# Three seams between the layers of a four-layer attention kernel, held banks for the statistics, and the order of the last tokens' products

## The chip, the cores and the metric

The kernel runs on one core of a Trainium2 chip. Its time is the device time of one execution in microseconds (us): the median of three runs is given, and a profile of one further execution. Engines are called as in the profile: PE (TensorE), DVE (VectorE), ACT (ScalarE), POOL (GpSimd), SP (the queue that issues DMAs).

## What is computed

The input x is four images of 56 x 56 pixels with 256 channels, float32. Four layers follow one another, each x = x + mixer(gn(x)), where gn is a group normalisation over 32 groups of channels and all pixels of an image. The core of the reference, cut:

```python
# layer 0: every pixel attends to its 7x7 neighbours, zero padding, 8 heads of 32
logits = einsum('ndhw,ndkhw->nkhw', q, unfold(k)) * scale
out = einsum('nkhw,ndkhw->ndhw', softmax(logits), unfold(v)) ; out @ wo.T + bo
# layer 1: all 3136 pixels of an image against each other
A = exp(5 * (xn xn' - rowmax)); A = A * (1 - eye); A = A / A.sum(-1)
diff = rowsum * (x W_aff) - (A x) W_aff ; leaky(layernorm(diff))
# layer 2: 7x7 neighbourhood attention clamped at the borders, 4 heads with
# dilation 1 and 4 with dilation 2, a relative position bias per head
# layer 3: attention within 7x7 windows of the image shifted by 3 pixels,
# a relative position bias and a mask of -100 between parts that don't touch
```

## The kernel before

The layers run one after another over all four images; the residual stream and the values go through DRAM between them. The kernel proper is the function `direct_blocks`. Layer 0 takes the span's first 712 us, layer 1 until about 2580, layer 2 until about 3238, layer 3 the rest. Near the end of a layer its units carry steps of the next one, as "fill".

**Who sets the order.** In layers 0 and 2 a scheduler orders the instructions of every engine by their dependences, unless an `issue_after` ties one to another. In layer 1 the order on PE and DVE, in layer 3 that on PE, DVE, ACT and POOL, is the order of the code (`manual_schedule`, called in `run`, L2304). SP issues its DMAs from one queue.

**Attention units, layers 0 and 2** (`attend_pairs`, L1062). A unit is a group of query pixels with all 8 heads. PE makes the logits (L1075) in two halves s0 and s1; DVE adds mask or bias to the one (L1082) and ACT takes its exp (L1083); ACT takes the exp of the other (L1085) and POOL multiplies it by the mask's exp (L1086). The next turn of the loop then issues, for the unit before ("held"): `both`, in which POOL adds the two key halves into b (L1095); the fill steps; the products (L1104): e with the values vp, then b with a matrix of ones for the sums; and `done`: a reciprocal on DVE, ACT's watch of it (`no`, L998), and the multiplication into attn on DVE (L1263, L1977 to L1983). The products go into a PSUM bank with tag o (two banks), which `gather` takes when the unit is made, before its logits; the gather also issues the DMAs of vp (L1967 in layer 2). Sixteen products of 32 columns count as x32 in the timeline.

**Rows.** Layer 0 has 32 rows r, each of seven pixel rows of an image and four units (`stream`, L1293; `balanced`, L1054, spreads the steps over them); the last three rows carry the first tokens of layer 1 instead. Layer 2 has 16 rows r of fourteen pixel rows and eight units: four column groups i, each with m = 0 and m = 1 (`stream`, L2014). Each row projects the row before (`project_out`; PE L952, DVE L2008 and L896) and prepares the next one: `normalise_act` (L942) on ACT or `normalise` (L945) on DVE, projections of queries and keys (L952), values (`value_tiles`, L979, evacuated at L983).

**Statistics** of the group norm (`group_stats`, L901): DVE aggregates (L910), PE sums over the group's channels (`mean`, L914), ACT squares and copies, PE sums again (`scale`, L921 and L922), POOL takes the root. `step_stats` issues one of these steps per unit. Their PSUM columns are 508 to 511 of `spare[0]`, the o bank that the newest unit has just taken; where `spare` is empty, a bank with tag m.

**First tokens of layer 1** (`first_tokens`, L1357). The first image's pixels in seven parts go through load, normal, lengths, values and unit_length; `plan` (L1419) puts these into the fill of layer 0's last three rows, thirteen lists.

**Last tokens of layer 1.** 3136 is 24 blocks of 128 and 64 more. These 64 against the rest are made by `rest_products` (L1609), three units per image; L1615 multiplies on 64 rows of the array, L1619 on 64 columns. PSUM tags in layer 1: s0, s1, o (2 banks), v (2), m (1), t (1). `add_up` evacuates a v bank.

**Masks of layer 3** (`table_steps`, L2060) are made within layer 2: four masks, each two DVE adds (L2072) of `found`, which is gathered by DMA, an exp on ACT (L2074) and one or three stores to DRAM (m3d).

**Layer 3** (`layer3`, L2091) loads the weights and m3, prepares row 0 and 1, makes both rows' values (three blocks of L979 each, in two steps), projects row 0, prepares row 2 and enters its loop `attend_quads` (L1004).

Of the kernel before, what the change touches and what calls it, by code (L numbers as in the profile page):

```python
# [24 lines left out]
FP = mybir.dt.float32  # L25
# [805 lines left out]
def direct_blocks(ctx: ExitStack, tc: tile.TileContext, d: dict, watch):  # L831
# [69 lines left out]
    def group_stats(l, b):  # L901
# [10 lines left out]
        def mean():  # L912
            pm = spare[0][:, 508:510] if spare else ps_m()
# [5 lines left out]
        def scale():  # L919
            pm = spare[0][:, 510:512] if spare else ps_m()  # L920
# [48 lines left out]
    def value_tiles(v, a, c, n, xn, w, bias, dst):  # L969

        t0, t1 = c * n // P, (c + 1) * n // P if (c + 1) * n < T else -(-T // P)
        pm = ps_m()
        sizes = [min(P, T - t * P) for t in range(t0, t1)]
        mine = sizes[2 * a:2 * a + 2]
        for j, k in enumerate(mine):
            first = (2 * a + j) * P
            for h in range(CC):
                for i in range(0, k, HD):
                    nc.tensor.matmul(pm[i:i + HD, j * C:(j + 1) * C], lhsT=xn[:, h, first + i:first + i + HD], rhs=w[:, h, :],  # L979
                                     start=(h == 0), stop=(h == CC - 1))  # L980
        for k in sorted(set(mine)):
# [72 lines left out]
    def balanced(units, steps, free):  # L1054

        n = len(units)
        for i, w in enumerate(units):
            mine = free[i] + steps[i * len(steps) // n:(i + 1) * len(steps) // n]
            w["fill"] = lambda mine=mine: [f() for f in mine]
            yield w  # L1060

    def attend_pairs(pool, units):  # L1062
# [4 lines left out]
        def logits(w):  # L1067
# [9 lines left out]
            for a in range(2):  # L1077
# [3 lines left out]
                if a == 0:  # L1081
                    newest[:] = [nc.vector.tensor_tensor(parts(ev), parts(sv), w["mask"], ALU.add)]  # L1082
                    nc.scalar.activation(ev, ev, AF.Exp)  # L1083
# [5 lines left out]
        def both(w):  # L1089

            nk, nq = w["nk"], w["nq"]
# [6 lines left out]
        def products(w):  # L1098
            nk, nq = w["nk"], w["nq"]
            for k in range(2):  # L1100
                for i, (_, _, v) in enumerate(w["quads"]):
                    for u in range(2 - k):
                        for j in range(4):
                            nc.tensor.matmul(  # L1104
                                w["o"](k, i)[j * HD:(j + 1) * HD], lhsT=ones[:nk, :HD] if k else v(j, u),
                                rhs=w["b"][j // 2][:nk, j % 2, i * nq:(i + 1) * nq] if k else
                                w["e"][j // 2][:nk, j % 2, (2 * i + u) * nq:(2 * i + u + 1) * nq],
                                start=(u == 0), stop=(u == 1 - k))

        held = None  # L1110
        for w in units:
# [4 lines left out]
            if held:  # L1116
                products(held)
                held["done"]()
            held = w
        both(held)  # L1120
        products(held)
# [21 lines left out]
    def layer0(early, big, pool, begin_layer1):  # L1143
# [85 lines left out]
        def pair(r, t):  # L1229
# [11 lines left out]
            def gather():  # L1241
                box["o"] = psum_tile("o", 2)
                spare[:] = [box["o"]]
# [24 lines left out]
            def quad(hq):  # L1268
                def keys(j, u):
# [6 lines left out]
                 for a in range(2)]  # L1276
            return dict(quads=[quad(0), quad(1)], nk=nk, nq=nq, mask=m[0], emask=m[1], first=gather, done=finish,
                        o=lambda k, i: box["o"][:, (2 * i + k) * nq:(2 * i + k + 1) * nq])
# [14 lines left out]
        def stream():  # L1293
# [10 lines left out]
            for r in range(NIMG * NB0):  # L1304
# [8 lines left out]
                if g > 2 or g == 0:  # L1313
                    for i in range(3):
                        free[i].insert(0, step_stats)
                attns[r] = pool.tile([P, CC, BT], FP, tag="attn", name="attn0")
                if r < ALONE:
                    yield from balanced([pair(r, t) for t in range(NTC)], steps, free)
                    continue
# [37 lines left out]
    def first_tokens(few, keep, brief):  # L1357
# [5 lines left out]
        nc.vector.memset(xw[:, :, C:], -1.0)  # L1363
# [14 lines left out]
        def normal(c):  # L1378
            m, n, x = part(c)
            sq = box["sq"] = brief.tile([P, CC, 512], FP, tag="sq", name="sq1")  # L1380
            for h in range(CC):
                normalise_act(x[:, h], x[:, h], known(1, 0), h)
# [25 lines left out]
        def unit_length(c):  # L1408
# [7 lines left out]

        v0, v2 = lambda c: values(c, 0), lambda c: values(c, 2)
# [3 lines left out]
            [(load, 1), (normal, R)],  # L1421
            [(load, 2), (lengths, R), (normal, 0)],
            [(load, 3), (v0, R), (unit_length, R), (lengths, 0)],
            [(v0, 0), (normal, 1), (v2, 0)],
            [(load, 4), (unit_length, 0), (lengths, 1)],
            [(v0, 1), (normal, 2)],
            [(load, 5), (v2, 1), (unit_length, 1), (lengths, 2)],
            [(v0, 2), (normal, 3), (v2, 2)],
            [(unit_length, 2), (lengths, 3)],
            [(v0, 3), (normal, 4)],  # L1430
# [4 lines left out]
    def layer1(early, big, pool, first, late, next_layer):  # L1435
# [173 lines left out]
        def rest_products(b, q, e, own, at):  # L1609
            po = psum_tile("o", 2)  # L1610
            for i in range(4):
                pv = [psum_tile("v", 2) for a in range(2)]
                for a in range(2):
                    half = slice(a * REST, (a + 1) * REST)
                    nc.tensor.matmul(pv[a][:, :C + 1], lhsT=e[half, i * P:(i + 1) * P], rhs=xw[half, NB, :], start=True, stop=True)  # L1615
                for a in range(2):
# [812 lines left out]
```

## Time and profile before

| | us |
|---|---|
| median of 3 runs (lowest, highest) | 3749.66 (3749.12, 3750.91) |
| profiled execution | 3749.95 |
| its span, first to last instruction | 3748.2 |
| mean granted PE clock, of full | 0.996 |
| PE idle in gaps of 0.4 us and more | 80.1, of it 13.6 before the first matmul |
| DMA | 304.94 MB, 81 GB/s |

Lines of the timeline have the start from the span's beginning, the duration from the first to the last of a run of like instructions, the engine and source line, output and inputs by name, the count, and in brackets the idle time of the engine before, with the instruction that ended it. Float32 matmuls leave two records each. Ends of matmuls are modelled, so durations of neighbours overlap a little.

### The profile page before, as it was taken

The numbers are of one execution on the slowest core, as the hardware profiler recorded it, in microseconds if no ns is written. First come the engines' busy times: TensorE is split into PE (matmuls) and PEld (weight loads), VectorE is DVE, ScalarE is ACT, GpSimd is POOL, SyncE is SP. The second block draws the span as 40 slices with busy tenths as digits, with TensorE's granted clock in tenths as the row PEclk, the third lists the DMA queues.
The fourth block names the chain that finished last, engine by engine and source line by source line (L and its number), as shares of the span: only waits on it lengthen the run. The fifth ranks groups of instructions, "written<-read, shape, count | busy, mean of one in ns | idle before, by whom it ended". The sixth has DMA issues, their size and how long they took to land. (4 is left out here: it accounts for less than half of the span.)

```text
span 3748.2 us, 112333 instructions
## 1 busy us (share of the span) xinstructions
PE 3658.8 (98%) x48826; PEld 2477.5 (66%) x48826; DVE 2203.5 (59%) x4188; ACT 1472.0 (39%) x3125; POOL 1812.2 (48%) x1966
## 2 busy tenths in 40 slices
PE   8999999999999999999999999999999999999998
PEld 4666666677776777767777667775666666555554
DVE  5787776544445444554444643445776777777776
ACT  5666666322222222222222222223666666444443
POOL 4777787522234222352222511123777777555555
PEclk9999999999999999999999999999999999999999
DMA  6554444300011000100000000002444444544443
GB/s 224 165 162 135 134 130 139 114 7 24 23 29 35 16 19 19 29 28 23 19 19 24 30 10 10 11 20 83 134 133 138 134 129 118 157 128 135 134 132 100
DMA packets 278039, 304.94 MB, mean 81 GB/s; under 512 B 33624, under 2 KB 268764, under 8 KB 277084
## 3 DMA queue, kind: packets, MB, share of 16 engines
q1 hardware_dynamic: 275680, 297.43, 26.1%
q8 instruction: 385, 6.31, 0.7%
q0 software_dynamic: 1568, 0.16, 0.1%
q14 instruction: 118, 0.97, 0.1%
q10 hardware_dynamic: 288, 0.08, 0.0%
HBM read 205.04 MB, written 92.55 MB: 79 GB/s over the span
## 5 line engine op out<-in xcount | busy, mean ns | idle before, releaser
L1576 DVE TENSOR_TENSOR acc<-acc,ps_v 128x257 f32<-128x257 f32 x1104 | 463.5, 422 | 782.2 <-PE ps_v L1654 753.6
L1654 PE MATMUL ps_v<-xw,e 128*128 128x257 f32 x2208 | 611.0, 381 | 3.4 <-DVE xnT L1521 2.2
L1649 PE MATMUL ps_o<-xw,at 128*128 128x257 f32 x2208 | 609.0, 379 | 0.0
L1544 PE MATMUL ps_s<-xnT,xd 128*128 128x512 f32 (+3 forms) x1344 | 571.4, 548 | 3.9 <-DVE xnT L1521 3.9
L1638 ACT COPY at<-ps_t 128x512 f32<-128x512 f32 (+3 forms) x332 | 170.3, 513 | 961.0 <-PE ps_t L1635 960.7
L1654 PEld LDWEIGHTS ps_v<-xw,e 128*128 128x128 f32 x2208 | 413.4, 189 | 144.6 <-issue 83.2
L1095 POOL TENSOR_TENSOR b<-e 126x336 f32<-126x336 f32 (+5 forms) x512 | 498.3, 993 | 6.9
L1649 PEld LDWEIGHTS ps_o<-xw,at 128*128 128x128 f32 x2208 | 419.1, 190 | 60.1
L952 PE MATMUL ps_m<-xn,w_wqkv 128*32 128x392 f32 x4096 | 376.9, 497 | 4.6 <-ACT kE L1908 3.2
L1537 POOL TENSOR_SCALAR xd<-xnT,vec 128x128 f32<-128x128 f32 x192 | 116.0, 613 | 478.3 <-PE ps_s L1544 478.2
L1547 ACT ACTIVATE e<-ps_s 128x512 f32<-128x512 f32 x336 | 185.3, 552 | 355.3 <-PE ps_s L1544 352.1
L1544 PEld LDWEIGHTS ps_s<-xnT,xd 128*128 128x128 f32 x1344 | 225.4, 191 | 141.4 <-issue 126.2
L1086 POOL TENSOR_TENSOR e<-e,m0t 126x672 f32<-126x672 f32 (+3 forms) x128 | 238.6, 1864 | 165.5 <-ACT e L1085 133.2
L1086 POOL TENSOR_TENSOR e<-e,bias 119x784 f32<-119x784 f32 (+5 forms) x128 | 239.6, 1872 | 157.6 <-ACT e L1085 157.1
L1104 PEld LDWEIGHTS ps_o<-e,vp 124*32 124x32 f32 (+3 forms) x8192 | 200.5, 110 | 101.2 <-issue 81.6
L998 ACT ACTIVATE no<-rs 128x168 f32<-128x168 f32 (+2 forms) x256 | 94.0, 367 | 409.8 <-DVE rs L1973 192.2
L952 PEld LDWEIGHTS ps_m<-xn,w_wqkv 128*32 128x32 f32 x4096 | 124.7, 110 | 179.9 <-issue 129.4
L1973 DVE RECIPROCAL rs<-ps_o 128x196 f32<-128x196 f32 (+2 forms) x128 | 175.7, 1372 | 104.1 <-PE ps_o L1104 104.1
L1104 PE MATMUL ps_o<-e,vp 124*32 124x112 f32 (+3 forms) x8192 | 229.8, 248 | 3.5 <-POOL e L1086 2.9
L1083 ACT ACTIVATE e<-e 126x672 f32<-126x672 f32 (+5 forms) x256 | 219.7, 858 | 14.3 <-DVE e L1082 2.1
L1085 ACT ACTIVATE e<-ps_s 126x672 f32<-126x672 f32 (+5 forms) x256 | 206.1, 805 | 5.0 <-PE ps_s L1075 5.0
L979 PE MATMUL ps_m<-w_wqkv,xn 128*32 128x256 f32 x3136 | 196.8, 381 | 2.1 <-DVE v L983 1.6
(223 smaller groups left out, 5952.3 us busy)
## 6 DMA issues: line engine op xcount, KB each, us to landing
x<-xr SPq DMA_DIRECT2D x64, 392.0 KB
x<-in_x SPq DMA_DIRECT2D x53, 448.0 KB
x<-x SPq DMA_DIRECT2D x60, 392.0 KB
xr<-x SPq DMA_DIRECT2D x60, 392.0 KB
vd<-v SPq DMA_DIRECT2D x72, 256.0 KB
xr<-in_x SPq DMA_DIRECT2D x32, 392.0 KB
xr<-x SPq DMA_DIRECT2D x28, 448.0 KB
x<-xr SPq DMA_DIRECT2D x28, 448.0 KB
```

What stands on the lines that cost most here:

```text
L952: nc.tensor.matmul(pm[j * HD:(j + 1) * HD, :n], lhsT=w[:, h, col + j * HD:col + (j + 1) * HD], rhs=rhs(h), start=(h == 0), stop=(h == CC - 1))
L979: nc.tensor.matmul(pm[i:i + HD, j * C:(j + 1) * C], lhsT=xn[:, h, first + i:first + i + HD], rhs=w[:, h, :], start=(h == 0), stop=(h == CC ...
L1083: nc.scalar.activation(ev, ev, AF.Exp)
L1085: nc.scalar.activation(ev, sv, AF.Exp)
L1086: nc.gpsimd.tensor_tensor(parts(ev), parts(ev), w["emask"], ALU.mult)
L1095: nc.gpsimd.tensor_tensor(w["b"][a][:nk, :, :2 * nq].rearrange("p h (i c) -> p h i c", i=2), ev[:, :, :, 0, :], ev[:, :, :, 1, :], ALU.add)
L1104: nc.tensor.matmul(w["o"](k, i)[j * HD:(j + 1) * HD], lhsT=ones[:nk, :HD] if k else v(j, u), rhs=w["b"][j // 2][:nk, j % 2, i * nq:(i + 1) ...
L1544: nc.tensor.matmul(s[:, :n], lhsT=xd[j][:, h, :], rhs=xnT[:, h, first * P:last * P], start=(h == 0), stop=(h == CC - 1))
L1547: nc.scalar.activation(e[:, :n], s[:, :n], AF.Exp, scale=5.0)
L1576: nc.vector.tensor_tensor(acc[:, i, :], acc[:, i, :], pv[:, :C + 1], ALU.add)
L1649: nc.tensor.matmul(out[j][:, :C + 1], lhsT=e[:, col(i)] if i == j else at[:, col(i)], rhs=xw[:, i, :], start=(i == j), stop=(i == NB - 1))
L1654: nc.tensor.matmul(pv[:, :C + 1], lhsT=e[:, col(i)], rhs=xw[:, j, :], start=True, stop=True)
```

## The change

- `group_stats`: mean and scale write columns 508 to 511 of the held unit's o bank, after that unit's products and before its done (`then` and `after` instead of fill steps).
- `alone`: three units of layer 0's last rows and the four m = 1 units of layer 2's last row have no POOL pre-add; their sums are made by 16 instead of 8 matmuls with ones over e.
- `first_tokens`: loads are issued two units before their use, the memset of xw's last column is a step of the plan, normal is tied behind the exp of the newest unit, and later steps are packed into fewer lists.
- `rest_products`: the order of the two kinds of products, and banks t and m beside v.
- `table_steps`: each mask's adds are tied behind the logit add of the row's last unit.
- layer 2 and 3: a new `layer3_ahead` is opened in layer 2. In row 14 (r = n - 2) it loads row 0 of layer 3 and the three parts of w_qkv, normalises rows 0 and 1 on ACT and loads one half of the first mask; row 14 projects out in units 4 to 7 instead of 2, 3, 6, 7. The six value blocks of layer 3's rows 0 and 1 are fill of units 0, 1, 4 and 5 of row 15, and of the tail. Layer 3 itself starts with the gather of row 0.

```diff
 def mean():
-    pm = spare[0][:, 508:510] if spare else ps_m()
+    pm = spare[0](0) if spare else ps_m()
 def scale():
-    pm = spare[0][:, 510:512] if spare else ps_m()
+    pm = spare[0](1) if spare else ps_m()
...
 def both(w):
+    if w.get("alone"):
+        return
 def products(w):
+    alone = w.get("alone")
     for k in range(2):
         for i, (_, _, v) in enumerate(w["quads"]):
-            for u in range(2 - k):
+            n = 1 if k and not alone else 2
+            for u in range(n):
...
     if held:
         products(held)
+        spare[:] = [held["spare"]]
+        for step in w.get("after", ()):
+            step()
+        spare.clear()
         held["done"]()
     held = w
 both(held)
+for step in tail:
+    step()
 products(held)
...
 # layer 0's units
+    alone=r == ALONE - 1 and t == 3 or r == ALONE and t == 2 or r == NIMG * NB0 - 1 and t == 3,
+    spare=lambda i: box["o"][:, 508 + 2 * i:510 + 2 * i],
...
 # first_tokens
-    for h in range(CC):
-        normalise_act(x[:, h], x[:, h], known(1, 0), h)
+    with tc.issue_after(newest[1].ins):
+        for h in range(CC):
+            normalise_act(x[:, h], x[:, h], known(1, 0), h)
...
 plan = [
     [(load, R), (load, 0)],
-    [(load, 1), (normal, R)],
-    [(load, 2), (lengths, R), (normal, 0)],
-    [(load, 3), (v0, R), (unit_length, R), (lengths, 0)],
+    [(load, 1)],
+    [(weights, 0), (load, 2), (normal, R)],
+    [(load, 3), (lengths, R), (normal, 0)],
+    [(v0, R), (unit_length, R), (lengths, 0)],
     [(v0, 0), (normal, 1), (v2, 0)],
-    [(load, 4), (unit_length, 0), (lengths, 1)],
-    [(v0, 1), (normal, 2)],
-    [(load, 5), (v2, 1), (unit_length, 1), (lengths, 2)],
-    [(v0, 2), (normal, 3), (v2, 2)],
-    [(unit_length, 2), (lengths, 3)],
-    [(v0, 3), (normal, 4)],
+    [(load, 4), (unit_length, 0), (lengths, 1), (v0, 1)],
+    [(normal, 2), (v2, 1)],
+    [(load, 5), (unit_length, 1), (lengths, 2), (v0, 2)],
+    [(normal, 3), (v2, 2)],
+    [(unit_length, 2), (lengths, 3), (v0, 3), (normal, 4)],
     [(v2, 3), (unit_length, 3), (lengths, 4), (normal, 5)],
     [(v0, 4), (v2, 4), (unit_length, 4), (lengths, 5), (v0, 5), (v2, 5), (unit_length, 5)]]
...
 def rest_products(b, q, e, own, at):
     po = psum_tile("o", 2)
+    def by_column(i, banks):
+        for a, bank in enumerate(banks):
+            pv = psum_tile(*bank)
+            half = slice(a * REST, (a + 1) * REST)
+            nc.tensor.matmul(pv[:, :C + 1], lhsT=e[half, i * P:(i + 1) * P], rhs=xw[half, NB, :], start=True, stop=True)
+            found.append((i, a, pv))
+    def add():
+        for i, a, pv in found:
+            add_up(b, 8 * q + 4 * a + i, pv, (nc.vector.tensor_copy, nc.scalar.copy)[a])
+        found.clear()
+    found, pair, others = [], [("v", 2)] * 2, [("t", 1), ("m", 1)]
+    by_column(0, pair)
+    by_column(1, others)
+    add()
     for i in range(4):
-        pv = [psum_tile("v", 2) for a in range(2)]
-        for a in range(2):
-            half = slice(a * REST, (a + 1) * REST)
-            nc.tensor.matmul(pv[a][:, :C + 1], lhsT=e[half, i * P:(i + 1) * P], rhs=xw[half, NB, :], start=True, stop=True)
-        for a in range(2):
-            add_up(b, 8 * q + 4 * a + i, pv[a], (nc.vector.tensor_copy, nc.scalar.copy)[a])
         for a in range(2):
             nc.tensor.matmul(po[a * REST:(a + 1) * REST, :C + 1], ...)
-        tick()
+        if i % 2:
+            tick()
+    by_column(2, others)
+    by_column(3, pair)
+    add()
+    for _ in range(2):
+        tick()
...
 # layer 2's rows
+    if r == n - 4:
+        q[n - 2], q[n - 1] = begin_layer3(0)
 if r:
-    for u, step in zip((2, 3, 6, 7), project_out(r - 1)):
+    for u, step in zip((4, 5, 6, 7) if r == n - 2 else (2, 3, 6, 7), project_out(r - 1)):
         work[u].append(step)
-for u in (1, 4, 5):
-    work[u].insert(0, step_stats)
+if r == n - 2:
+    work[4].append(begin)
+    for u in range(1, 4):
+        work[4 + u].append(lambda u=u: steps3[u]())
+if r == n - 1:
+    for u in (0, 1, 4, 5):
+        work[u].append(lambda: values3.pop(0)())
...
+w["after"] = [step_stats] * (u in (1, 4, 5))
...
-attend_pairs(pool, stream())
+attend_pairs(pool, stream(), [lambda: values3.pop(0)()] * 2)
...
 # masks
-    nc.vector.tensor_tensor(m[:, :, sl], ...)
+    with tc.issue_after(newest[0].ins):
+        nc.vector.tensor_tensor(m[:, :, sl], ...)
...
+steps = [lambda: (load(0), load_weight(2)), lambda: load_weight(1),
+         lambda: (prepare(0, later), load_weight(0)), lambda: (prepare(1, later), load_mask())]
...
 # layer3
-prepare(0)
-prepare(1)
-for r in range(2):
-    for step in values(r):
-        step()
+gather(0)
 for step in project_rows(0):
     step()
-prepare(2)
+with tc.issue_after(newest[0].ins):
+    prepare(2)
```

## The prediction

> **What bounds the kernel now.** I read the page's first part, then the waits of TensorE, then the timelines of the three seams between layers, because a nearly full engine can only win where it stands still or runs slowly.
>
> ```profile
> PE 3658.8 (98%) x48826; PEld 2477.5 (66%) x48826; DVE 2203.5 (59%) x4188; ACT 1472.0 (39%) x3125; POOL 1812.2 (48%) x1966
> ```
>
> TensorE (PE) is the bound everywhere but in a few stretches. The change neither adds nor removes more than some 3 us of matmul, so what can be won is its idle time (80 us in gaps over 0.4 us, 13.6 of it before the first matmul), slow clock after long gaps, and dearly ordered matmuls. The waits (us in total, times, longest):
>
> ```profile
> PE ps_o L1104 <- POOL b L1095: 6.2, 11, 1.2
> PE ps_o L921 <- DVE attn L1263: 5.1, 6, 0.9
> PE ps_m L952 <- DVE attn L1263: 4.5, 4, 3.8
> PE ps_o L921 <- ACT no L998: 4.3, 4, 1.2
> PE ps_s L1075 <- DVE e L1082: 3.9, 4, 1.5
> PE ps_m L952 <- ACT kE L1908: 3.2, 1, 3.2
> ```
>
> Every row of these meets the change. In the PE timeline of the first and second seam (start, duration, instruction, count, idle before):
>
> ```profile
> 627.87 1.12 PE L1075 MATMUL ps_s<-q,kI 32*126 32x84 f32 x32 [1.13 <-DVE e L1082]
> ...
> 633.53 2.84 PE L952 MATMUL ps_m<-attn,w_wo 128*32 128x392 f32 x16 [3.82 <-DVE attn L1263]
> ```
> ```profile
> 2614.31 4.29 PE L952 MATMUL ps_m<-xn,w_wqkv 128*32 128x392 f32 x32 [3.22 <-ACT kE L1908]
> ```
>
> Both long gaps are followed by matmuls at about half speed: 16 of L952 take 1.52 us in row 15 and 2.84 here; 32 take 2.84 just before 2611 and 4.29 after it. In the windows view (PE, PEld, DVE, ACT, POOL busy, PE clock, DMA share, GB/s) the first seam has the clock at 0.83, and layer 2's last row, on the way into the third seam, has full clock but POOL at 97%:
>
> ```profile
> 626.00:649.00 23.00, 16.10 (x318) 11.24 (x308) 14.11 (x23) 18.64 (x34) 13.55 (x13) 0.83 0.70 214
> 3196.00:3211.00 15.00, 12.92 (x352) 8.92 (x352) 12.37 (x18) 7.95 (x17) 14.49 (x13) 1.00 0.37 114
> ```
>
> [...] at the last-token products a step within a form is 0.214 us, the first after a switch 0.27 to 0.32, the last before one 0.31 to 0.37. [...] the mask adds (L2072) take 0.84 us at best and 1.3 to 2.5 beside POOL. [...]
>
> **Part 1, statistics in held banks.** Mean and scale matmuls (L914, L921) now use columns 508 to 511 of the o bank of the unit whose products were just issued, instead of the newest unit's bank, for which they wait until DVE or ACT has read the unit before. Layer 0: 0.77 + 5 x 0.86 = 5.1 us go. Layer 2: 1.05 + 1.04 + 1.05 = 3.1 go (a fourth, 1.20, is counted in the second seam). Late next: the unit's reciprocal waits some 0.3 us longer for the bank, on a DVE that idles 1.7 us per unit in most of layer 2 (timeline at 3166 to 3172); I charge nothing. Bounds: 0 to 0.3 us for 24 units, so +7 at the very worst. The ACT reads of the two columns move behind the products too; nothing but the next statistics step waits for them.
>
> **Part 2, first seam (613 to 719).** DVE stood before the 3.82 gap because its square-add waited 3.19 us for ACT, and ACT waited for a DMA; DVE's memset waited for a vd store. Now loads are issued two units ahead, the memset comes two units later, and normalise_act is placed behind the unit's exp. Excess there: 1.13 + 3.82 + 1.28 (slow L952) + 0.56 = 6.8, all gone if the load is early; 0.62 + 1.33 + 0.48 + 0.88 = 3.3 at 644 to 651, half of which I count (1.65), since the later steps are packed into fewer units; about 5.3 after that, none counted. Three units are now "alone": no POOL pre-add, but 16 instead of 8 sum matmuls, 0.55 + 0.40 + 0.55 = +1.5. Net -7.0; between -10 and -3.
>
> **Part 3, products of the last tokens** (12 units, 67.1 us in all: 4.9, 5.7 or 6.2, 6.1 per image).
>
> ```profile
> 719.28 0.66 PE L1619 MATMUL ps_o<-xw,at 128*64 128x257 f32 x4
> 719.92 0.70 PE L1615 MATMUL ps_v<-xw,e 64*128 64x257 f32 x4
> ```
>
> Now L1615 and L1619 alternate, four records (two side-by-side pairs) each, so each pays a switch in and out: 0.32 + 0.31 = 0.63, the spacing seen. After: eight L1615 records (0.32 + 2 x 0.214 + 0.31 = 1.06), sixteen L1619 (1.92), eight L1615 (1.06): 4.04 per unit. 12 x 4.04 + 4 x 0.58 (own columns, one unit per image) = 50.8. The v, t and m banks must be free: I leave 0.74 x 3 + 0.2 x 8 = 3.8 of bank waits and 1.0 because t has one bank, giving 55.6: -11.5. Between -13 and -7 (the transposes queued behind the products wait for bank t; up to 0.4 per unit).
>
> **Part 4, second seam (2580 to 2660).**
>
> ```profile
> 2611.04 3.15 DVE L2072 TENSOR_TENSOR m<-found,t 98x392 f32<-98x392 f32 x4 [2.61 <-DMA found<-looked_up]
> ...
> 2627.71 3.84 DVE L2072 TENSOR_TENSOR m<-found,t 98x392 f32<-98x392 f32 x2 [0.20 <-ACT e L1085]
> ```
>
> The masks wait for a gather, ACT waits 5.36 us for the masks with the keys' evacuation queued behind, and PE waits 3.22 for that. Idle and slow clock: 3.22 + 1.59 + 0.92 + 0.74 + 0.28 + 0.97 + 1.49 = 9.2, plus the statistics wait 1.20. Now one mask (two adds, one exp, its stores) follows the last unit's logit add in each of rows 1 to 4. There DVE has 3.9 us of work in a unit of 4.84 and gets 1.74 to 3.8 more; over two units that fits or misses by up to 2. Queued behind on DVE are the reciprocal and the next logit add, for which PE waits. I take 0.45 per row (bounds 0 and 2): -10.4 + 1.8 = -8.6; between -10.4 and -3.
>
> **Part 5, third seam (3161 to 3244).**
>
> ```profile
> 3202.63 0.39 PE L1104 MATMUL ps_o<-b,ones 124*32 124x112 f32 x4
> ...
> 3203.72 0.58 PE L1104 MATMUL ps_o<-b,ones 124*32 124x112 f32 x12 [0.71 <-POOL b L1095]
> ```
>
> Row 15 (3196 to 3230.3) is paced by POOL: 15.1 us of e and b per four units, PE having 11.6. Four of its units are now alone (two per four): POOL 15.1 - 3.4 = 11.7, PE 11.6 + 0.9, plus two of the moved value blocks (5.5 us for six, L979) 1.84 = 14.3. DVE becomes level: 10.85 + 2.4 (residual adds and statistics) + 1.1 (value evacuation) = 14.35. So the row takes 28.8 instead of 34.3: -5.5. In the tail, waits of 1.0 us for POOL go, two blocks come (+1.84), and layer 3's opening loses its value stretch (3238.0 to 3243.9, 5.9): -5.0. Row 14: the output projection moves to its second half: -2.7 in the first, DVE at 10.85 + 4.8 = 15.65 against 14.8 in the second, +0.85. Sum -12.4. ACT takes the two normalisations (2.2 us each; ACT is busy 53%). Against it I set one lost cover in each of the four half rows, of the size of the wait above: +2.8. Net -9.6; between -13 and -4. The SP queue is what may fail: in row 14 it is almost full already,
>
> ```profile
> 3171.64 9.70 SPq L1967 DMA_DIRECT2D vp<-vd  x12
> ```
>
> and gets seven more issues of 0.4 us, for about 30.4 of 31.6 us.
>
> **The sum.** -5.1 - 3.1 - 7.0 - 11.5 - 8.6 - 9.6 = -44.9. The profiled execution took 3749.95 us (span 3748.2 plus 1.75 around it), 0.3 above the median of 3749.66: 3705.
>
> **The rivals.**
> - Seams half filled: waits return in new places (masks 1.5 per row, the packed first-token steps, SP in row 14). -3 - 11.5 - 5.1 - 4.4 - 3.1 - 4 = -31: 3719. For it: DVE is level with PE in the new rows. Against: the long gaps came from DMA waits that go.
> - The product order gains nothing, because bank t or v is late in each unit: -44.9 + 10 = 3715. Against: the v waits so far cost 0.7 at most.
> - Better: the 5.3 us late in the first seam go too and covers hold: 3696.
> - Slower: SP falls behind in rows 14 and 15. If each of the 16 units gets its gathered values a unit late, each costs up to one unit, 3.8 us: 61 - 45 = +16, 3766. It decides once issues per unit exceed the unit's time; 30.4 of 31.6 says it doesn't, by little, and only in row 14.
> - The change doing nothing: the instruction order shows the moves made; only the waits could stay as they are (3750).
>
> **Numbers.** Forecast (3700 to 3712) 0.48; half filled or no gain from order (3712 to 3726) 0.27; better (3690 to 3700) 0.16; between 3726 and 3742: 0.04; no change 0.02; slower 0.03. I leave out half of the better end (below 3694) and what lies above 3725, so the range is 3694 to 3725. A difference of 0.2% (7.5 us) is about what a measurement of this kernel can tell from none: faster 0.95, same 0.02, slower 0.03.
>
> **What would show it.** L921 without waits; no PE gap over 1.5 us between 620 and 3240 and no clock dip at 626 or 2614; last-token units of 4.1 to 4.9 us; row 15 in under 30 us with POOL below 85%; layer 3's first logits some 10 us nearer to row 15's end. Wrong would be: L1075 waiting over 1 us behind a mask in rows 1 to 4, L1104 waiting for vp in rows 14 and 15, or L1605 waiting for bank t.

## The result, and the profile after

The changed kernel takes 3717.87 us (median of six runs, 3716.25 to 3720.84), beside 3750.64 for the kernel before in the same series: a ratio of 0.9909, 95% interval 0.9898 to 0.9919. The forecast was 3705 with a range of 3694 to 3725. So the sign and the range held, and some 12 us of the expected 45 did not come. The profiled execution of the changed kernel is the slowest of its six (3720.84 us, span 3719.0), so the trace accounts for 29.1 us rather than 32.8.

PE's idle time in all fell from 80.1 us to 64.1. (The 80.1 given above for gaps of 0.4 us and more is all of its idle time; gaps of that size alone make 70.8 us before and 54.1 after.)

The first part of the page after, the engines and the PE waits that answer to those of before (us in total, times, longest; L1080 was L1075, L1113 was L1104, L1102 was L1095):

```profile
PE 3645.2 (98%) x48938; PEld 2480.5 (67%) x48938; DVE 2197.2 (59%) x4176; ACT 1479.4 (40%) x3137; POOL 1802.9 (48%) x1952
```
```profile
PE ps_m L952 <- DVE attn L1277: 4.3, 7, 1.0
...
PE ps_o L1113 <- DMA vp<-vd: 3.9, 7, 1.0
...
PE ps_m L1406 <- DVE sq L1398: 3.5, 4, 1.2
...
PE ps_m L981 <- DVE xr L2044: 2.0, 1, 2.0
...
PE ps_o L1113 <- POOL b L1102: 1.8, 6, 0.7
...
PE ps_s L1080 <- DVE e L1087: 0.8, 2, 0.5
```

The rows of L921 with attn and with no are gone, the long waits of L952 for attn (3.8) and kE (3.2) too, and POOL's b fell from 6.2 to 1.8. Three larger rows are new: the products L1113 wait for gathered values, 3.9 us; the sums L1406 wait for DVE's squares, 3.5 us; and one of the moved value blocks (L981) waits 2.0 us for DVE's residual add. The squares lie in the first seam, the other two in the third, and in these two seams the forecast failed.

**Where the time went.** I took the start of the same matmul in both traces at eight places: the logits of the units (256 of them, numbered from 0), the first L1603 (L1586 before) as the start of layer 1, the first projection of layer 2, the first logits of layer 3. The difference between two places is what a stretch won or lost. Each column of such a table rests on one execution of each kernel.

| stretch | forecast | trace |
|---|---|---|
| start to unit 0 | 0 | +0.65 |
| layer 0 to unit 116 (statistics) | -5.1 | -7.85 |
| first seam, unit 116 to layer 1 | -7.0 | +2.64 |
| layer 1 (last tokens' products) | -11.5 | -11.97 |
| second seam, layer 2's start to unit 137 | -10.4 | -12.52 |
| units 137 to 239 (masks +1.8, statistics -3.1) | -1.3 | +0.64 |
| third seam, unit 239 to layer 3 | -9.6 | -1.25 |
| layer 3 and the end | 0 | +0.55 |
| sum | -44.9 | -29.11 |

A "dip" below is a stretch in which PE's granted clock is half (0.50 in the clock records of both traces). Between 25 us and the loop of layer 3 both traces have five dips, of 23.9 us in all, at different places, so the 29.1 us do not come from fewer dips.

**First seam.** The PE timeline of the changed kernel there:

```profile
622.52 1.52 PE L952 MATMUL ps_m<-attn,w_wo 128*32 128x392 f32 x16 [0.88 <-DVE attn L1277]
...
630.94 0.38 PE L1406 MATMUL ps_m<-ones,sq 128*128 128x1 f32 x2 [1.20 <-DVE sq L1398]
...
637.04 1.02 PE L1406 MATMUL ps_m<-ones,sq 128*128 128x1 f32 x8 [0.92 <-DVE sq L1398]
...
639.09 2.01 PE L1080 MATMUL ps_s<-q,kI 32*126 32x84 f32 x32
641.03 6.11 PE L1418 MATMUL ps_m<-w_waff,xnT 128*128 128x256 f32 x16
```

The gap of 3.82 us is down to 0.88, as intended. Then come new gaps, none over 1.2 us, and yet the clock dips, for 6.8 us from 639.1 on: L1080 takes 2.01 us instead of 1.12, and 16 of L1418 take 6.11 where 16 of them took 3.82 before (L1404).

**Third seam.** SP's queue at the end of row 14 (lines of SPq give the issue time), then PE in row 15:

```profile
3151.98 0.64 SPq L2167 DMA_DIRECT2D w_wqkv<-in_wqkv  x1
...
3155.86 0.71 SPq L2167 DMA_DIRECT2D w_wqkv<-in_wqkv  x1
...
3157.64 0.45 SPq L2205 DMA_DIRECT2D m3a<-m3d  x1
3158.20 3.10 SPq L2002 DMA_DIRECT2D vp<-vd  x4
3161.40 0.46 SPq L2047 DMA_DIRECT2D x<-xr  x1
3161.96 4.34 SPq L2002 DMA_DIRECT2D vp<-vd  x4
3167.92 0.37 SPq L2041 DMA_DIRECT2D xr<-x  x1
```
```profile
3165.23 0.35 PE L1113 MATMUL ps_o<-e,vp 126*32 126x84 f32 x8 [1.04 <-DMA vp<-vd]
...
3173.18 0.40 PE L1113 MATMUL ps_o<-e,vp 124*32 124x112 f32 x8 [0.80 <-DMA vp<-vd]
...
3177.10 2.01 PE L1080 MATMUL ps_s<-q,kI 32*126 32x84 f32 x32
3179.04 2.84 PE L952 MATMUL ps_m<-attn,w_wp 128*32 128x392 f32 x16
```

SP's own waits from 3150 to 3175 show what it stood for (us in total, times, longest):

```profile
SPq L2041 <- DMA x<-xr: 1.5, 1, 1.5
SPq L2002 <- DMA m3a<-m3d: 1.1, 1, 1.1
```

Four gathers that take 3.1 us to issue take 4.34 here, because one of them stands 1.1 us until the load of the half mask (3157.6) has landed. Then SP stands from 3166.3 to 3167.9 until the residual's store (3161.4) has landed, since the reload xr behind it needs that buffer. The gathers of the next units queue behind all this. PE waits for them piece by piece and the clock dips again (2.84 for 16 of L952 instead of 1.52). Window, busy times by engine as in the prediction, and PE's clock of 0.50 before the last two numbers:

```profile
3175.18:3182.00 6.82, 6.55 (x91) 3.91 (x89) 2.83 (x5) 1.86 (x4) 2.97 (x3) 0.50 0.66 209
```

**The same order in other traces.** Four of the kernels below (t_old, t_hyb, t_notie, t_v0) change only the first tokens and have the changed kernel's instructions in the same order in rows 14 and 15, on SP as well. In all five traces PE waits 3.0 to 4.2 us for vp in the third seam. But a dip follows in three of them only. With it the third seam is crossed at -1.25 (the changed kernel), -1.23 (t_old) and -0.89 (t_hyb), without it at -4.38 (t_notie) and -3.67 (t_v0):

```profile
3164.00:3213.00 49.00, 42.48 (x1049) 26.01 (x1044) 37.78 (x56) 20.56 (x45) 25.23 (x19) 1.00 0.50 154
```

This is t_notie's row 15 up to layer 3, at full clock throughout. A single crossing of this seam can thus differ by 3.5 us without any edit to it.

### The profile page after: what moved, and what is told of

The parts are those of the page before. It is cut to its first block, busy times and chain, and to the rows that moved or that the text cites. A ratio compares the mean times of both kernels' runs of the same rounds, so it can differ in the third digit from the quotient of the medians.

```text
span 3719.0 us, 112489 instructions
## 1 busy us (share of the span) xinstructions
PE 3645.2 (98%) x48938; PEld 2480.5 (67%) x48938; DVE 2197.2 (59%) x4176; ACT 1479.4 (40%) x3137; POOL 1802.9 (48%) x1952
## 4 chain that ended last, share of the span: by engine, by line
PE 90%; DVE 4%; POOL 1%; DMA 1%; issue 1%; ACT 1%; SPq 0%; DVEq 0%; ACTq 0%; POOLq 0%
PE ps_m L952 19%; PE ps_o L1683 14%; PE ps_s L1561 14%; PE ps_v L1688 13%; PE ps_m L981 7%; PE ps_o L1113 6%; PE ps_s L1080 6%; PE ps_t L1669 3%; PE ps_o L1040 2%; PE ps_s L1024 1%; PE ps_m L1526 1%; DMA vp<-vd 1%; POOL b L1102 1%; PE ps_m L1418 1%; PE ps_m L1754 1%
## 5 line engine op out<-in xcount | busy, mean ns | idle before, releaser
L1102 POOL TENSOR_TENSOR b<-e 124x448 f32<-124x448 f32 (+5 forms) x498 | 484.7, 994 | 7.2 <-PE ps_o L1113 0.3
L952 PE MATMUL ps_m<-xn,w_wqkv 128*32 128x392 f32 x4096 | 374.3, 494 | 2.3 <-PE ps_s L1080 1.1
L1113 PEld LDWEIGHTS ps_o<-e,vp 124*32 124x32 f32 (+3 forms) x8192 | 198.0, 110 | 104.4 <-issue 85.3
L952 PEld LDWEIGHTS ps_m<-xn,w_wqkv 128*32 128x32 f32 x4096 | 124.3, 109 | 176.5 <-issue 128.7
L1113 PE MATMUL ps_o<-e,vp 124*32 124x112 f32 (+3 forms) x8192 | 227.6, 248 | 4.2 <-DMA vp<-vd 3.9
L981 PE MATMUL ps_m<-w_wqkv,xn 128*32 128x256 f32 x3136 | 197.6, 381 | 3.8 <-DVE xr L2044 2.0
```

What stands on the lines that cost most here:

```text
L952: nc.tensor.matmul(pm[j * HD:(j + 1) * HD, :n], lhsT=w[:, h, col + j * HD:col + (j + 1) * HD], rhs=rhs(h), start=(h == 0), stop=(h == CC - 1))
L1102: nc.gpsimd.tensor_tensor(w["b"][a][:nk, :, :2 * nq].rearrange("p h (i c) -> p h i c", i=2), ev[:, :, :, 0, :], ev[:, :, :, 1, :], ALU.add)
L1113: nc.tensor.matmul(w["o"](k, i)[j * HD:(j + 1) * HD], lhsT=ones[:nk, :HD] if k else v(j, u), rhs=w["b"][j // 2][:nk, j % 2, i * nq:(i + 1) ...
```

## The experiments

Each kernel below is the changed one with one edit, unless said otherwise. "Crossing" is the same difference between two places as in the table, kernel before = 0, from one trace of each. The runs were made in four series, and the kernel before, measured again in each, has medians from 3749.96 to 3753.81 us, so a few us between medians of different series tell little. By the ratios only v_back is clear of the changed kernel (0.9898 to 0.9919); the intervals of all others overlap with that. The held banks, the order of the last tokens' products and the alone units were not undone singly: what is said of them is read from the traces.

**t_old: the first tokens as before.**
```diff
-            with tc.issue_after(newest[1].ins):
-                for h in range(CC):
-                    normalise_act(x[:, h], x[:, h], known(1, 0), h)
+            for h in range(CC):
+                normalise_act(x[:, h], x[:, h], known(1, 0), h)
```
with the old plan and the memset at its old place.

> The changed kernel with the first tokens' steps as before: old plan, memset at the start, no tie of normal (the alone units stay). If the redone plan is worth what the prediction said (8.5 us without the alone units), this kernel is 8.5 us slower than the changed one, about 3726. The traces say otherwise: from the first logits of unit 116 to layer 1 the changed kernel lost 2.6 us of its lead, 1.5 of it by the alone units, so the plan is worth about -1: then this kernel is within 2 us of the changed one, and layer 1 starts with a lead of 4 to 7 us over the kernel before.

Measured: 3714.23 us (3713.03 to 3715.8), ratio 0.9897 (0.9881 to 0.9914). The first seam is crossed at -0.70 instead of +2.64. The redone plan is not worth 8.5 us; without it the kernel is 3.6 us faster by the medians (the two intervals overlap). The places of the memset and the loads were not tested apart from the plan. The -0.70 itself is less than equal orders differ by here (see below); POOL's wait of 1.16 us at 697 is gone in this kernel too, which fits the alone units.

**t_notie: only the tie of normal undone.**
```diff
-            with tc.issue_after(newest[1].ins):
-                for h in range(CC):
+            if True:
+                for h in range(CC):
```

> The changed kernel without the tie of normal behind the newest unit's exp; plan and memset as changed. Theory that the tie is what makes PE wait for the squares (L1406 behind DVE sq, 3.5 us in four waits, and the clock dips that follow, some 6 us): the waits go and the layer-1 start comes 4 to 9 us sooner, 3709 to 3714. Rival, that the packed lists make them: no more than 1 us of change. Second rival, that the normalisation then blocks ACT as before: slower by up to 4.

Measured: 3716.16 us (3715.0 to 3717.56). The crossing is +2.54, as in the changed kernel. The tie does what it was put there for: without it the long gap is back (3.98 us before L952, behind attn), and the waits for the squares are gone. But the sum is the same. That speaks against the first theory: in these traces the tie only exchanges one long gap for several short ones.

**t_hyb: the tie for two parts only.**
```diff
+            if c in (NC4, 0):
+                with tc.issue_after(newest[1].ins):
+                    both_halves()
+            else:
+                both_halves()
```

> The changed kernel with normal tied only for the first two parts (the 64 last tokens and the first block), the others free. If the tie removes the one long gap and in later parts makes PE wait for the squares, the gap of 4 us stays away, the waits at 663 and 678 go, and layer 1 starts 2 to 5 us sooner relative to unit 116 than in the changed kernel (which loses 2.6 there). If the packed lists make the waits, no change beyond the 3 us by which equal code differed here.

Measured: 3718.2 us (3716.92 to 3721.02), crossing +1.23. The waits at 663 and 678 went, and a gap of 3.14 us came at 624, where logits wait for an ACT exp that stands behind a free normalisation. No gain stands out.

**t_v0: values ahead of the lengths in the plan.**
```diff
-            [(unit_length, 2), (lengths, 3), (v0, 3), (normal, 4)],
+            [(unit_length, 2), (v0, 3), (lengths, 3), (normal, 4)],
```
and likewise in four more lists; some values move one list forward.

> The changed kernel with the first tokens' values put ahead of the lengths in five lists of the plan, so that PE has 1 us of value products while DVE adds the squares. If the waits for the squares and the clock dips behind them are what the new plan loses, the waits at 636, 663 and 678 (2.4 us) go and at least one dip with them: layer 1 starts 3 to 6 us sooner relative to unit 116 (where the changed kernel loses 2.3 in the mean of six traces, -0.3 to 4.1). If the packing delays the chain of steps itself, the waits come back elsewhere: within 1.5 us of 2.3.

Measured: 3717.11 us (3715.33 to 3720.04), crossing +1.46. All but one (1.25 us at 629) of the waits for the squares gave way to others at the same matmul, 2.54, 2.72 and 1.30 us, for a bank with tag m that ACT (the first, the values) or DVE (the other two, in unit_length) had not read yet. This agrees with the rival, that in this plan the chain of steps is late whatever is first.

**l_act: layer 3's loads from ACT's queue.**
```diff
-            nc.sync.dma_start(out=w_qkv[:, :, k * C:(k + 1) * C],
+            nc.scalar.dma_start(out=w_qkv[:, :, k * C:(k + 1) * C],
...
-            nc.sync.dma_start(out=m3, in_=m3d[:, 0, :4].rearrange("p h w k -> p h (w k)"))
+            nc.scalar.dma_start(out=m3, in_=m3d[:, 0, :4].rearrange("p h w k -> p h (w k)"))
```

> The changed kernel with the three weight thirds and the half mask issued from ACT's queue instead of SP's. If SP's issue time makes the gathered values late in rows 14 and 15 (seven more issues, four of them these), the waits of L1113 for vp (3.9 us) and the clock dip after them (2.5) shrink by over half: 3 to 6 us faster, 3712 to 3715. If it is the transfers' share of the DMA engines (85% busy from 3160 to 3165), the waits stay within 1 us: 3717 to 3719.

Measured: 3721.62 us (3720.65 to 3722.31), ratio 0.9917 (0.9901 to 0.9934): slower by the medians. Both forecasts missed, for a reason that neither had: ACT stands in its queue between these issues, up to 3.48 us before an exp, and PE gets a gap of 4.78 us at 3152.5. After it row 15 has no wait for vp at all. This doesn't yet show that SP's issues made the gathers late, since SP could also catch up while PE stood. From unit 248 to layer 3 this kernel wins 4.0 us where the changed one wins 1.0, but t_notie wins 3.75 there with all loads on SP.

**l_late: loads written into row 15.**
```diff
+                    for k, u in enumerate((2, 3, 6)):
+                        work[u].append(lambda k=k: steps3[4 + k]())
```

> The changed kernel with two of the weight thirds and the half mask loaded in units 2, 3 and 6 of row 15 instead of units 5 to 7 of row 14. If the lot of SP work and transfers at the end of row 14 makes the gathers late, whichever of the two, the waits for vp before unit 251 go: 4 to 7 us faster, 3711 to 3714. If the moved output projection does it (its store must land before the next load behind which the gathers queue), at most 2 us. If row 15 is as tight as row 14, the waits only move: no change.

Measured: 3716.1 us (3715.65 to 3716.33), third seam -1.28, as before the edit. The loads did not move: the instruction order shows them in row 14 still, presumably because the scheduler takes a DMA that nothing holds as early as it can (tied loads do move, see l_tied). The run tells nothing on the cause, but something else: see the clock below.

**l_tied: the same, each load behind a gather of its unit.**
```diff
+                    def tied(k):
+                        with tc.issue_after(gathers[0].ins):
+                            steps3[4 + k]()
```

> As the kernel with late loads, but now the loads really stand in row 15: each is queued on SP behind the gathers of units 2, 3 and 6 (there the scheduler had moved them forward to the end of row 14 again). If the four loads make the values of units 247 to 251 late (SP time or transfers), their waits of 3.4 us and the clock dip go: 4 to 6 us between unit 239 and layer 3 (which the changed kernel crosses with a gain of 1.2). If the store and reload of the residual (1.5 us of waiting on SP) is the cause, 0 to 1.5.

Measured: 3714.07 us (3712.25 to 3714.9), ratio 0.9899 (0.9883 to 0.9916), third seam -6.47 instead of -1.25. On PE, DVE, ACT and POOL this kernel has the instructions of the changed one in the same order; SP alone differs, in where three loads (two weight thirds and the half mask) stand in its queue. Not all of the 5.2 us is their price: the trace has no dip in this seam. Beside the two traces of the old queue that have none either, l_tied wins 2.1 and 2.8 us. That part is where the last unit of row 14 ends: from unit 239 to 248 the three kernels with moved loads (l_tied, best1, best2) win 2.5 us, all others with the projection at its new units 0.8 at most. The rest, 2.4 to 3.1 us, goes with the dip that followed the waits in three of five traces of the old queue; of the three kernels with moved loads two have no dip there and best1 a short one (1.7 us lost). The longest waits left in row 15 of l_tied:

```profile
3173.33 0.58 PE L1113 MATMUL ps_o<-b,ones 124*32 124x112 f32 x12 [0.71 <-POOL b L1102]
...
3184.12 0.38 PE L1113 MATMUL ps_o<-e,vp 85*32 85x98 f32 x8 [0.54 <-DMA vp<-vd]
```

**p_slots: row 14's output projection at its old units.**
```diff
-                    for u, step in zip((4, 5, 6, 7) if r == n - 2 else (2, 3, 6, 7), project_out(r - 1)):
+                    for u, step in zip((2, 3, 6, 7), project_out(r - 1)):
```

> The changed kernel with row 14's output projection back in units 2, 3, 6 and 7. Theory that the projection's store, queued late, holds the reload and with it the gathers of row 15: the wait of SP for the store goes, row 15 begins up to 2 us sooner, but the first half of row 14 gives back 2.5: within 1.5 us of the changed kernel. Rival, that the loads alone hold SP: 2 to 3 us slower.

Measured: 3716.35 us (3714.83 to 3717.79), third seam -3.95. The gain of 2.5 in row 14 is gone, as expected, but the waits for vp in rows 14 and 15 are gone too, although all loads are still at the end of row 14. So the loads alone do not make the gathers late. This fits the queue as the cause, when loads, the late store and the wait for it meet; but row 14 is also 2.5 us longer here than in l_tied, in which SP can catch up, and that was not separated. Nor does the absence of the waits show in the time: from unit 248 to layer 3 it wins 3.95, as l_tied does (3.97), but t_notie, which waits 2.7 us for vp there and has no dip either, wins 3.75.

**v_back: the value blocks back at layer 3's start.**
```diff
-                if r == n - 1:
-                    for u in (0, 1, 4, 5):
-                        work[u].append(lambda: values3.pop(0)())
...
+        for step in first3:
+            step()
         gather(0)
```

> The changed kernel with the six value blocks back at the start of layer 3; loads, normalisation, projections and alone units stay. By the prediction the blocks are free in row 15: this kernel would be 5.9 - 1.8 = 4 us slower. If PE rather than POOL paces row 15 now that gathers, alone units and values share it, the blocks cost what they save: within 1.5 us.

Measured: 3731.98 us (3728.87 to 3733.47), 14 slower. Most of it is no measure of the move: the values' tile vt has one buffer, so the second row's evacuation waits 11.5 us for the first row's stores to land, the second of which SP issues behind loads of masks and weights (at 3214.5), and PE has a gap of 10 us. What can be read is row 15: from unit 239 to 255 it loses 4.15 us without the value blocks, 3.85 with them; both traces have the dip there. In that row the blocks cost nothing that shows.

**u_masks: the masks free again.**
```diff
-                with tc.issue_after(newest[0].ins):
+                if True:
                     nc.vector.tensor_tensor(m[:, :, sl], ...)
```

> The changed kernel with the masks free again instead of tied behind a logit add. If the tie is what frees the second seam, the lead of 12.5 us won between layer 2's first projection and unit 137 falls to 1 to 4, and the 0.6 to 3.7 us that units 137 to 200 lose go: 7 to 11 us slower, 3725 to 3729. If the scheduler would place the masks well by itself now, no change.

Measured: 3723.91 us (3721.28 to 3726.34), 6.0 slower. The second seam is crossed at -6.1 instead of -12.5, and units 137 to 168 lose nothing instead of 3.7. The size is below what I gave: half of the seam's gain is there without the tie. Of that 1.2 are the statistics. Some 3.2 more are two dips that the kernel before has in this seam (2613.9 and 2634.4) and this one has not, although PE's gap before L952 is back (2.73 us after 3.22). So in this seam too a part of what was won is whether a dip follows a gap.

**best1: two mends.** The old first tokens (t_old) and l_tied's loads in one kernel.

> The changed kernel with the old steps of the first tokens and with the loads of layer 3 queued behind gathers of row 15: two mends of the change together. If the two losses are independent they add: 3.6 and 3.8 us, 3710 to 3711. If the dips at the seams only move, 3712 to 3714.

Measured: 3709.46 us (3708.97 to 3710.28), ratio 0.9885 (0.9869 to 0.9902). 8.4 us under the changed kernel by the medians, with all four runs below all six of that one; the sum of the two mends by themselves was 7.4, so they add as far as this can tell. Beside l_tied, from which it differs by the old first tokens alone, it is 4.6 us faster.

**best2: two more.** All late loads behind the last gather of row 15, and the tie for two parts of the old plan.
```diff
-                    for k, u in enumerate((2, 3, 6)):
+                    for k, u in enumerate((7, 7, 7)):
```

> The better kernel (old steps of the first tokens, layer 3's loads behind row 15's gathers) with two more mends: all three late loads behind the gathers of row 15's last unit, where no gather follows them, and the tie of normal for the first two parts of the old plan. First mend: the waits for vp in row 15 (1.1, 0.3 and 1.2 us) go, 1 to 2.5 us between unit 248 and layer 3. Second: if the tie by itself removes the gap of 3.5 us at 622, layer 1 starts 2 to 4 us sooner after unit 116 (where the better kernel gains 2.4), less if the squares are then late: 3705 to 3708. If both only move the waits, 3708 to 3711.

Measured: 3709.88 us (3709.53 to 3711.16), ratio 0.9886 (0.9869 to 0.9902): no gain. The waits for vp fell from 2.6 us to 0.5, but a wait of 2.04 us of the last value block for DVE, which the changed kernel has too and best1 had not, took the place; at the first seam the gap at 622 went and one of 3.32 came at 625. From unit 248 to layer 3 best2 wins 4.0, best1 2.8, and the first seam takes 1.4 of it back.

## Why the prediction was right, and where it was not

Of the cases set out, the first rival came closest: seams half filled, 3719 us. It had the sum right by other parts than it named: the masks' waits were mild, the first seam gave nothing and the third almost nothing, layer 0 and the second seam gave more. That the total still lies in the range is in part luck: by the table the first and third seam missed the forecast by 18.0 us together, and layers 0 and 1 and the second seam gave 5.3 more than forecast.

**Statistics.** Right in kind, too small in layer 0: -7.85 for -5.1. The L921 waits of 0.77 to 0.86 went; what I left out is that, as I read the two traces, the late pair had also broken the order that the scheduler gave to the matmuls behind it. Before, the pair L921 and L922 stood within a run of L952, and the next unit's e and b products came interleaved by threes and ones and took 1.6 us (274.0 to 275.6); now they come in two runs and take 1.0. A new wait of 0.8 to 1.0 us for attn, three times, is the other side: the late next that I had named and charged with nothing. Layer 2's three waits gave -3.1, as forecast.

**First seam: the step that failed** is "all gone" together with "half of which I count". The 3.82 us gap went, and with it the slow L952. But I priced the packed plan as if fewer lists cost only the late gains, and put their own waits at nothing. Steps that had a unit between them now wait on each other (ACT's normalisation after the exp, then squares, DVE's sum, PE's lengths): 5.6 us of gaps of 0.25 us and more from 629 to 682, where the kernel before had 2.4 after its long one, and one more dip of the clock. The windows of the changed kernel, then of l_late and l_tied, which have the same order on PE, DVE, ACT and POOL (the number before the last two is the PE clock):

```profile
621.00:641.00 20.00, 16.45 (x398) 12.62 (x392) 15.88 (x24) 11.94 (x24) 16.89 (x15) 0.95 0.80 246
641.00:661.00 20.00, 19.88 (x265) 14.49 (x264) 12.07 (x19) 9.79 (x18) 14.73 (x14) 0.88 0.19 63
661.00:681.00 20.00, 18.10 (x329) 13.10 (x317) 13.53 (x19) 10.15 (x18) 12.80 (x11) 0.91 0.18 51
681.00:701.00 20.00, 18.67 (x214) 13.26 (x215) 14.44 (x23) 10.16 (x18) 10.68 (x9) 0.91 0.19 61
```
```profile
621.00:641.00 20.00, 16.54 (x384) 12.85 (x385) 15.85 (x26) 12.29 (x26) 16.96 (x16) 0.94 0.77 249
641.00:661.00 20.00, 19.50 (x315) 14.18 (x313) 13.41 (x18) 11.23 (x18) 15.89 (x15) 0.98 0.22 66
661.00:681.00 20.00, 17.09 (x269) 12.51 (x268) 15.31 (x23) 11.72 (x22) 14.01 (x12) 0.96 0.13 40
681.00:701.00 20.00, 19.66 (x222) 14.17 (x221) 11.52 (x18) 7.15 (x14) 10.96 (x12) 0.95 0.18 61
```
```profile
621.00:641.00 20.00, 16.96 (x378) 13.39 (x382) 14.36 (x23) 11.73 (x23) 16.97 (x16) 0.87 0.77 247
641.00:661.00 20.00, 19.88 (x254) 14.43 (x254) 12.13 (x19) 9.45 (x17) 12.64 (x12) 0.87 0.17 55
```

One minus the clock, times 20, summed over the four slices, is time lost to the clock: 7.0 us in the changed kernel, 3.4 in l_late, 8.8 in l_tied (its last two slices have 0.91 as well). They cross the seam at +2.64, -0.28 and +4.12. So the clock (5.4 us between the last two) covers the spread of 4.4 us between equal orders, and no single trace sizes an edit here to better than that. The kernel before, from which all crossings are counted, is one trace too. Over seven traces with the changed steps the mean is +2.3; the old steps have -0.7 and, in best1, -2.4. So the packed steps lose some 3 to 5 us against the old ones, which stand on two traces; which of the packing's waits costs it stays open.

**Last tokens' products.** Right. The twelve units take 54.7 us instead of 67.1, 0.9 under my 55.6; layer 1 gives -11.97.

```profile
715.54 1.96 PE L1647 MATMUL ps_o<-xw,at 128*64 128x257 f32 x16
```

Sixteen records in one run: 1.89 us to the next one in all twelve units (1.92 in the sum). The units take up to 0.9 us more than the 4.04 of the sum (4.62 with own columns). The trace has no idle time of PE in them, so it does not show the waits for banks that I had allowed for. One reading of the prediction was wrong: a step of 0.214 us within a form does not occur at these products before, where such a step takes 0.27 or 0.32; the products L1649 of the same width show 0.216 there, and the run of sixteen now 0.22.

**Second seam.** The sum was right (-8.8 to unit 168 with the masks' cost, -8.6 forecast), both terms being larger: the seam gave 2.1 more than the gaps I had added up, and the masks took 3.7 instead of 1.8. In eleven other traces with the tie the masks took 0.6 to 2.5, and the stretch gave -10.0 to -11.9, so this trace is the odd one and 1.8 was a fair price. The two adds of a mask run beside POOL, the first in 0.88 to 0.89 us, the second in 2.40 to 2.42 (median of all 1.65):

```profile
2665.42 3.22 DVE L2125 TENSOR_TENSOR m<-found,t 98x392 f32<-98x392 f32 x2
```

Before, four adds with no POOL instruction beside them took 0.84 to 0.85 us and the four beside POOL 0.89, 1.71, 2.52 and 1.41, where the prediction has 1.3 to 2.5. The instructions behind them on DVE slip as forecast; in u_masks, where the masks are free, the stretch from unit 137 to 168 loses nothing.

**Third seam: the steps that failed** are two. The first is the cover that I set against it, "one lost cover in each of the four half rows", +2.8, with SP "almost full already", 30.4 of 31.6 us. I had made the late gathers a rival for the slower side only, with a chance of 0.03 and a price of 3.8 us in all of 16 units. They came, as the sign of being wrong that I had named, in a mild form in three units, and took 5.2 us where the dip followed (the changed kernel beside l_tied), 2.1 to 2.8 where none did. The sum of issue times left out that SP also stands: 1.6 us for the store of the moved projection, 1.2 among the gathers behind the loads. (The 31.6 is not row 14 as traced either: 34.9 us lie between the logits of units 240 and 248 before.)

The second is the row's time as the largest of the engines' sums, 28.8 us for row 15. In l_tied, without a dip, its first seven units take 28.5 us; seven eighths of my sum of PE work are 25.0, and before they took 26.9. POOL's b waits of 0.2 to 0.7 us, vp of 0.2 to 0.5 and stretched runs make the 3.5 between: in this row, with PE busy for 26.3, DVE for 22.8 and POOL for 21.7 of the 28.5 us, the time is not the largest of the engines' sums. After the seven units the same holds. From unit 255 to layer 3 the trace gives -5.1, which is what I had for the tail and the opening (-5.0), but the last eighth of the row (7.4 us before) should have given some 3.7 more. There the value block waits 2.0 us for DVE's residual add, and in most traces the projection 0.9 us for attn.

## What to carry to other kernels

Where a step is moved into a row that is already even, add up each queue's waits as well as its issues: here a gather stood 1.1 us until a load had landed and a reload 1.5 us until a store had, with eight gathers behind it. Removing one long gap by a tie was no gain where the steps behind it were packed so closely that several short gaps followed (the first seam is crossed at +2.64 with the tie, +2.54 without). And before you size an edit of a few us next to such gaps, take several traces of the same instruction order, of the kernel before too, and look in each whether the clock dipped: a seam without any edit differed by 3.5 us between traces.

## What the runs showed of the hardware that I had not expected

- The clock dipped without a long gap before it: in the changed kernel gaps of 1.20, 0.56 and 0.92 us within 8 us, with matmuls of one column (L1406) among the work between them, were followed by a dip (639.07 to 645.90). In t_v0 gaps of 1.25, 0.55 and 0.78 us at the same place were not (clock 1.00 from 621 to 651), nor was the gap of 2.73 us in u_masks.
- In the clock records of the kernel before and of the changed one, from 25 to 3700 us, the clock is 1.00 or 0.50. Each has five dips: before, of 6.83, 3.41, 3.41, 3.41 and 6.83 us, after, of 6.83, 3.41, 3.41, 6.83 and 3.41. Half of that, 1.7 or 3.4 us, is lost where PE has work throughout. The longest gap of PE that began in the 10 us before a dip was of 0.71 to 3.82 us. A gap of such a size alone does not tell that a dip follows: after the one of 1.56 us before 2591.4, in the kernel before, the clock stays at 1.00 until 2613.9.
- With loads in ACT's queue (l_act) ACT was idle for 3.48 us before the exp at 3155.5: the issue of the half mask, ahead of it in that queue, started at 3154.9 only. On SP the same four issues took 2.3 us in the changed kernel.
